# The first layer's turns: tap products in pairs, norms by VectorE's 32x32 transposes, TensorE's order fixed in the source

## The chip, the cores and the metric

The kernel runs on one core of one Trainium2 chip. The time is that of the device, in microseconds, for one launch. Engines are named as in the profile: PE is TensorE's matmuls, PEld its weight loads, DVE is VectorE, ACT is ScalarE, POOL is GpSimd, SP is SyncE, which issues DMAs here.

## The reference

The kernel computes a network of four attention layers over two images of 512 channels and 64x64 pixels in float32. Only the first layer matters here. It has eight heads of 64 channels, and each pixel attends to its 3x3 neighbourhood and to a pooled copy of the image at once. Cut to what is computed:

```python
x = group_norm(x)
q = l2norm(x @ W_q + b_q)                    # per head of 64 channels
qs = (q + query_embedding) * softplus(temperature)
k, v = split(x @ W_kv + b_kv);  k = l2norm(k)
local  = [sum_d qs * k[y + dy, x + dx] for 9 taps (dy, dx)]
pooled = qs @ l2norm(k_pool).T               # k_pool, v_pool from gelu(x @ W_sr) pooled by 4
a = softmax(concat(local, pooled))
a_local = a[:9] + q @ learnable_tokens + learnable_bias
out = (sum_taps a_local * v[y + dy, x + dx] + a[9:] @ v_pool) @ W_proj + b_proj
```

## The kernel before

Channels lie on the 128 partitions. The image's 512 channels are four chunks, its 4096 pixels four units of 1024, so the layer has 16 units for each image, numbered chunk by chunk. A chunk holds two heads. A block is 512 pixels (`TB`).

`Local.run` goes through turns i = -4 to 16. Each turn gives every stage another unit: keys are projected for unit i + 4, queries for i + 3, values and tap sums for i + 1 ("ahead"), attention is done for i, and the weighted sum of the nine neighbours for i - 1. A stage is a generator, and `in_turn` steps all of them round robin, one `yield` at a time; so the yields set the order of the source. The order in which each engine executes is not the source's: the tile framework's scheduler orders every engine's instructions, with the source's order as priority, and with what it takes to be ready. PSUM banks come from a pool (`bank()`, tiles called `mm`); who takes a bank next waits for the last reader of its content.

The stages, with the lines of before:

- `projections`: two 512-pixel blocks each of keys, queries and values: four matmuls of 128x128 by 512 for each (L134), ScalarE adds the bias and makes the squares.
- `norms`: four matmuls (L2276) sum the squares of up to four blocks over each head, with column groups of 32, so the rows of one PSUM bank hold two heads for each of the four. ScalarE copies them (L2279), TensorE transposes them (L2283, four times 128x128), VectorE takes inverse roots by Newton's steps on 32 columns (L2290 to L2298, into `wide`), TensorE transposes back (L2304), ScalarE copies (L2306).
- `normed`: a matmul spreads each head's scale over its 64 channels (L2318), VectorE multiplies keys (in the padded frame `kx`) and queries by it (L2326). Then `learned` makes the learnable part of the query (L2339).
- `tap_products`: VectorE multiplies the queries by the keys shifted by each of the nine taps, 128x1024 each (L2366), into a ring of three buffers `prods`.
- `tap_sums`: for each tap two matmuls of 128x32 (one for each block, L2379) sum a product over each head. Tap parity and block choose one of four column groups of 32 in one bank; ScalarE takes the exponentials.
- `attend`: scores against the pooled keys (L2411, two heads each), their exponentials (L2415), values (L2421), sums in halves added by GpSimd (L2426) and then over all (L2433, L2437), the reciprocal (L2458), and the local weights, which go to DRAM by the `rows` DMAs.
- `weigh`: for each tap a DMA brings the weights back, spread over channels (`rows` to `big` or `tap`), ScalarE copies them to PSUM (L2491), VectorE multiplies by the shifted values (L2499), GpSimd adds (L2504), and the sum goes to `yd` in DRAM (L2510).
- `fetch_output` and `output`: in the last turns the output projection reads `yd` back (L2199).

SyncE has one queue for these DMAs, in the order of its instructions. Turns 0 to 2 have no value blocks to project: units 0 to 3 of the values are made in turns -4 to -2 (the first chunk). Turns -4 to -1 only fill the pipeline, turns 12 and 13 project no keys, 13 no queries either, and 14 to 16 drain it and do the output. The pooled heads are worked out in turns -4 and -3.

Of the kernel before, what the change touches and what calls it, by code (L numbers as in the profile page):

```python
# [1914 lines left out]
class Local:  # L1915
# [9 lines left out]
    def __init__(self, net, X, Y, sp_scale, d, wp, yp, pp, ppt, pps):  # L1925
# [20 lines left out]
        self.prods = [whole.take([P, self.UT])] + [new([P, self.UT], f"prod{i}") for i in range(2)]  # L1946
# [19 lines left out]
        self.qn = new([P, self.UT], "qn")  # L1966
# [3 lines left out]
        self.wide = new([P, NT, P], "wide")  # L1970
# [12 lines left out]
        nc.gpsimd.memset(self.wide, 0.0)  # L1983
# [11 lines left out]
    def run(self):  # L1995


        self.nmean = self.net.stats[:, 0]
        xs = self.pooled_tokens()
        heads = self.pooled_heads(xs)  # L2000
        units = KC * self.UN
        unit = lambda u: u if 0 <= u < units else None
        self.pending = []
        for i in "qkv":
            self.fetch(i, 0)
        for i in range(-4, units + 1):
# [12 lines left out]
            values = ([ahead] if i >= self.UN - 1 and ahead is not None  # L2019
                      else {-4: [0], -3: [1, 2], -2: [3]}.get(i, []))  # L2020
            stages.append(self.projections(k, q, values, streams))
            stages.append(self.normed(ended))
            if i < -2:
                stages.append(islice(heads, 12 if i == -4 else None))
            if i == units - 3:
                stages.append(self.fetch_output())
            if i > units - 3:
                stages.append(self.output(i - units + 2))
            in_turn(*stages)

        self.nc.sync.dma_start(self.next_w, self.d["w_q1"].rearrange("(kc p) o -> p kc o", p=P))
        in_turn(self.output(KC - 1))
# [136 lines left out]
    def fetch_output(self):  # L2169

        for _ in range(3):

            yield
# [6 lines left out]
    def output(self, c4):  # L2180
# [4 lines left out]
        toks = ([self.prods[0], self.prods[1], self.prods[2], self.qs[(units - 2) % 3]] if c4 % 2  # L2185
# [46 lines left out]
    def projections(self, uk, uq, uvs, streams):  # L2232
# [23 lines left out]
        for step in range(10):  # L2256
            if step >= 6:
                project((uk, uq)[step // 2 - 3], "kq"[step // 2 - 3], step % 2)
            if step % 3 == 0 and values:
# [6 lines left out]
    def norms(self, streams, ended):  # L2266
# [11 lines left out]
        rows = wp.tile([P, TB], F32, name="n_rows")  # L2278
        nc.scalar.copy(rows, ps)  # L2279
        yield  # L2280
        ps = self.bank()
        for t in range(NT):
            nc.tensor.transpose(ps[:, t * P:(t + 1) * P], rows[:, t * P:(t + 1) * P],  # L2283
                                self.net.ident)


        sums = ps.rearrange("p (t s r) -> p t s r", t=NT, s=4)
        n, a = (sums[:, :, :, 2 * i:2 * i + 2] for i in range(2))
        y = wp.tile([P, NT, 4, 2], F32, name="roots")
# [4 lines left out]
        for i in range(3):  # L2294
            nc.vector.tensor_tensor(a, n, y, ALU.mult)
            nc.vector.tensor_tensor(a, a, y, ALU.mult)
            dst = self.wide.rearrange("p t (s r) -> p t s r", s=4)[:, :, :, :2] if i == 2 else y
            nc.vector.scalar_tensor_tensor(dst, a, 1.5, y, ALU.add, ALU.mult)  # L2298
        yield
        yield  # L2300
        yield
        ps = self.bank()
        for t in range(NT):
            nc.tensor.transpose(ps[:, t * P:(t + 1) * P], self.wide[:, t, :], self.net.ident)  # L2304
        rows = wp.tile([P, TB], F32, name="n_rows")
        nc.scalar.copy(rows, ps)  # L2306
# [3 lines left out]
    def normed(self, ended):  # L2310

        nc = self.nc
        for _ in range(5):
            yield
        for which in "kq":
# [11 lines left out]
            yield  # L2327
        if mine:
# [27 lines left out]
    def tap_products(self, u):  # L2356
# [5 lines left out]
        qs = qs.rearrange("p (y x) -> p y x", x=W)  # L2362
        y = u % self.UN * self.UY
        for k in range(9):
            dy, dx = divmod(k, 3)
            self.nc.vector.tensor_tensor(  # L2366
                self.prods[k % 3].rearrange("p (y x) -> p y x", x=W), qs,
                self.kx[:, y + dy:y + dy + self.UY, dx:dx + W], ALU.mult)
            yield

    def tap_sums(self, u):
# [3 lines left out]

        def sums(k):
            for j in range(2):
                q = 2 * j + k % 2
                nc.tensor.matmul(ps[32 * q:32 * q + 32, :],  # L2379
                                 self.cst[:, C_TAPW + 16 - 2 * k:C_TAPW + 48 - 2 * k],  # L2380
                                 self.prods[k % 3][:, j * TB:(j + 1) * TB], start=(k < 2),
                                 stop=(k > 6))
# [15 lines left out]
    def attend(self, u):  # L2398
# [45 lines left out]
        yield  # L2444
        values(0)
        yield
# [5 lines left out]
        yield  # L2452
# [9 lines left out]
        nc.vector.tensor_tensor(el, el, self.lt.pop(u), ALU.add)  # L2462
        self.spread = self.rows()
# [237 lines left out]
```

## Time and profile before

| | us |
|---|---|
| median of 3 runs | 5164.23 (5158.23 to 5171.0) |
| the profiled execution, its own time | 5163.61 |
| span of the profiled execution | 5161.7 |
| mean granted TensorE clock | 0.979 |
| VectorE busy | 3067.8 (59%) |
| ScalarE busy | 1863.1 (36%) |
| first-layer turns -3 to 13, first image | 194.6 to 904.0 |

In the windows table a row is one stretch of time, with each engine's busy time and number of instructions, the granted clock (1.00 is full), the share of the DMA engines and what they moved. In a group's line come the source line, engine, operation, what is written and read, shapes and count, then the busy time and the mean duration of one in ns, then the engine's idle time just before them and what ended it. A logical float32 matmul shows as two records. Turns are cut here where the first L2276 of each starts: 194.6, 232.3, 256.9, 290.4, 326.9, 370.5, 419.7, 463.5, 508.3, 552.6, 599.0, 642.7, 686.8, 730.5, 774.5, 818.2 and 860.9 us for i = -3 to 13.

### The profile page before, as it was taken

To read this page: it belongs to the slowest core of one execution; us is meant where nothing else is said; L and a number is where in the kernel's file an instruction comes from. 1 tells how busy PE (TensorE), PEld (TensorE's weight loads), DVE (VectorE), ACT (ScalarE), POOL (GpSimd) and SP (SyncE) were. 2 spreads that over 40 slices of the span, in tenths; PEclk is the share of its full clock that TensorE was granted. 3 is DMA by queue.
4 is the path that set the end of the run, shared out by engine and by line. 5 is a ranking of instruction groups with operands and counts; after the bars stand their busy time and mean duration, and the time that the engine had idled before them with its cause. 6 is when DMAs were issued, how large, how long until landed. Compare 5 with 4: busy or idle time off the path is not lost. (4 is left out here: it accounts for less than half of the span.)

```text
span 5161.7 us, 48736 instructions
## 1 busy us (share of the span) xinstructions
PE 4898.0 (95%) x17299; PEld 2034.4 (39%) x17299; DVE 3067.8 (59%) x3986; ACT 1863.1 (36%) x3547; POOL 1844.2 (36%) x1216
## 2 busy tenths in 40 slices
PE   7999999899999999999999999998999999999998
PEld 3423332555334444433344333325543344444333
DVE  4266777644579633478732677776446795334766
ACT  1245565324323233322112555652343232333221
POOL 0035566500420045454500455555013201454554
PEclk9999999999999999999999999999999999999999
DMA  3025556600000000211110355565000000000111
GB/s 149 2 78 137 144 140 171 173 27 10 1 1 17 1 1 1 66 52 49 58 70 3 96 142 140 143 168 163 19 10 1 2 15 1 1 1 21 39 46 44
DMA packets 124752, 309.88 MB, mean 60 GB/s; under 512 B 20882, under 2 KB 33682, under 8 KB 122964
## 3 DMA queue, kind: packets, MB, share of 16 engines
q1 hardware_dynamic: 124500, 306.68, 21.0%
q8 instruction: 139, 2.28, 0.2%
q14 instruction: 113, 0.93, 0.1%
HBM read 258.11 MB, written 48.50 MB: 59 GB/s over the span
## 5 line engine op out<-in xcount | busy, mean ns | idle before, releaser
L134 PE MATMUL mm<-big,w 128*128 128x512 f32 x2496 | 1162.5, 610 | 9.2 <-DVE late L2458 9.2
L134 PEld LDWEIGHTS mm<-big,w 128*128 128x128 f32 x2496 | 455.9, 192 | 677.0 <-issue 559.0
L2504 POOL TENSOR_TENSOR late<-late,big 128x1024 f32<-128x1024 f32 x192 | 454.1, 2365 | 196.4 <-DVE big L2499 178.8
L1616 POOL TENSOR_TENSOR big<-big 128x512 f32<-128x512 f32 x224 | 277.3, 1270 | 219.8 <-ACT big L1607 219.8
L2426 POOL TENSOR_TENSOR late<-late 128x512 f32<-128x512 f32 x128 | 160.6, 1276 | 514.6 <-ACT late L2415 492.6
L2499 DVE TENSOR_TENSOR big<-big,mm 128x512 f32<-128x512 f32 x384 | 255.9, 683 | 124.5 <-ACT mm L2491 104.5
L2491 ACT COPY mm<-big 128x512 f32<-128x512 f32 x428 | 244.8, 593 | 174.0 <-DMA big<-rows 140.3
L1607 ACT ACTIVATE big<-mm,ed 128x256 f32<-128x256 f32 x512 | 193.6, 489 | 232.8 <-DVE top L1603 200.4
L2504 POOL TENSOR_TENSOR late<-late,tap 128x1024 f32<-128x1024 f32 x96 | 227.1, 2366 | 101.1 <-DVE tap L2499 97.8
L1420 POOL TENSOR_TENSOR wq<-prob 128x512 f32<-128x512 f32 x48 | 70.8, 1498 | 506.6 <-ACT prob L1417 506.6
L1871 PE MATMUL mm<-k,w 128*128 128x512 f32 x512 | 236.8, 606 | 12.3 <-DVE k L1864 7.3
L1603 DVE TENSOR_REDUCE top<-mm 128x1 f32<-128x512 f32 x256 | 159.1, 684 | 148.5 <-PE mm L1535 148.5
L134 PE MATMUL mm<-big,wq 128*128 128x512 f32 x512 | 235.2, 609 | 2.7 <-ACT off_t L1219 2.7
L2366 DVE TENSOR_TENSOR prod<-qs,big 128x1024 f32<-128x1024 f32 x192 | 230.7, 1217 | 8.7 <-PE tap L2379 7.0
L1191 PE MATMUL mm<-big,wo 128*128 128x512 f32 x512 | 234.7, 604 | 0.0
L1581 PE MATMUL mm<-w,big 128*128 128x512 f32 x512 | 234.5, 601 | 0.0
L1346 PE MATMUL acc<-big,diag 128*128 128x512 f32 x512 | 226.5, 601 | 4.6 <-ACT diag L1344 4.6
L1861 DVE RECIPROCAL psD<-psD 128x512 f32<-128x512 f32 x64 | 215.1, 3362 | 1.9
L969 POOL TENSOR_TENSOR group_stats<-group_stats,cst 128x1 f32<-128x1 f32 (+1 forms) x20 | 12.1, 621 | 570.2 <-DVE group_stats L968 538.7
L2379 PE MATMUL tap<-prod,cst 128*32 128x512 f32 x768 | 198.3, 602 | 8.9 <-DVE prod L2366 8.0
L134 PE MATMUL mm<-big,big 128*128 128x512 f32 x464 | 201.7, 594 | 0.5 <-DVE b_sr L1007 0.5
L1417 ACT ACTIVATE prob<-mm 128x512 f32<-128x512 f32 x256 | 133.0, 603 | 171.6 <-PE mm L1414 171.4
(410 smaller groups left out, 8477.2 us busy)
## 6 DMA issues: line engine op xcount, KB each, us to landing
big<-rows SPq DMA_DIRECT2D x428, 256.0 KB, 4.3
tap<-rows SPq DMA_DIRECT2D x212, 256.0 KB, 4.2
yd<-late SPq DMA_DIRECT2D x32, 512.0 KB, 2.9
lost_all<-lost SPq DMA_DIRECT2D x128, 128.0 KB, 3.1
out<-big SPq DMA_DIRECT2D x64, 256.0 KB, 2.0
big<-in_W_kv SPq DMA_DIRECT2D x8, 1024.0 KB, 9.4
rows<-late SPq DMA_DIRECT2D x64, 128.0 KB, 2.3
big<-yd SPq DMA_DIRECT2D x16, 512.0 KB, 5.1
```

The source lines that it names most:

```text
L134: self.nc.tensor.matmul(ps, w[:, kc, :], X[:, kc, blk * TB:(blk + 1) * TB], start=(kc == 0), stop=(kc == KC - 1))
L1191: nc.tensor.matmul(ps, w[:, kc, oc * P:(oc + 1) * P], att[:, kc, :], start=(kc == 0), stop=(kc == KC - 1))
L1346: nc.tensor.matmul(accs[b], dg, src[:, b * TB:(b + 1) * TB], start=(j == 0), stop=(j == 6))
L1581: nc.tensor.matmul(ps, X[:, kc, lo:lo + P], wv[:, kc, :], start=(kc == 0), stop=(kc == KC - 1))
L1616: nc.gpsimd.tensor_tensor(a, a, part, ALU.add)
L1861: nc.vector.reciprocal(psD, psD)
L1871: nc.tensor.matmul(ps, self.wo[:, kc, oc * P:(oc + 1) * P], qs[:, kc, :], start=(kc == 0), stop=(kc == KC - 1))
L2366: self.nc.vector.tensor_tensor(self.prods[k % 3].rearrange("p (y x) -> p y x", x=W), qs, self.kx[:, y + dy:y + dy + self.UY, dx:dx + W], A ...
L2379: nc.tensor.matmul(ps[32 * q:32 * q + 32, :], self.cst[:, C_TAPW + 16 - 2 * k:C_TAPW + 48 - 2 * k], self.prods[k % 3][:, j * TB:(j + 1) * ...
L2491: nc.scalar.copy(ps, part)
L2499: nc.vector.tensor_tensor(part.rearrange("p (y x) -> p y x", x=W), self.vx[:, y:y + self.UY // 2, dx:dx + W], ps.rearrange("p (y x) -> p y ...
L2504: nc.gpsimd.tensor_tensor(out, out, t, ALU.add)
```

## The change

All of it is in the class `Local`, the first layer. Tap products are made two at a time: one VectorE instruction of 128x2048 for two taps, its keys read through an access pattern that steps from one tap's shift to the next's, and its queries read twice; the ninth tap stays alone. The ring is now two buffers of two products. The tap sums follow in pairs. In `norms`, both sets of TensorE transposes and both ScalarE copies go; VectorE transposes the 32x32 blocks of the sums in place in PSUM, does the same thirteen steps, and transposes back into the buffer `sq[3]` (whose squares were read by then). `wide` goes, and `qn` moves to the large buffer. In turns 0 to 13 TensorE's instructions run in the source's order; the other engines are still ordered by the scheduler. The yields are moved: values are projected at steps 0, 2, 5 and 9, keys and queries at 4, 6, 7 and 8; `normed` begins two steps earlier and learns one step later; the values of the first score group come one step later and of the second one step earlier, the rows' DMA one step later, and the output's fetch after 7 steps rather than 3.

The lines of after that answer to those of before: sums of squares L2279, first VectorE transpose L2282, the steps L2285 to L2292, second transpose L2294, scale matmul L2306, multiply L2314, learnable part L2328, products L2353, tap sums L2380, scores L2404, values L2414, reciprocal L2450, tap multiply L2492, tap add L2497.

```diff
@@ run
-            in_turn(*stages)
+            if 0 <= i < units - 2:
+                with self.net.tc.manual_schedule(engines={mybir.EngineType.PE}):
+                    in_turn(*stages)
+            else:
+                in_turn(*stages)
...
@@ __init__
-        self.prods = [whole.take([P, self.UT])] + [new([P, self.UT], f"prod{i}") for i in range(2)]
+        self.prods = [new([P, 2, self.UT], f"prods{i}") for i in range(2)]
-        self.qn = new([P, self.UT], "qn")
+        self.qn = whole.take([P, self.UT])
-        self.wide = new([P, NT, P], "wide")
-        nc.gpsimd.memset(self.wide, 0.0)
...
@@ fetch_output
-        for _ in range(3):
+        for _ in range(7):
...
@@ projections
         for step in range(10):
-            if step >= 6:
-                project((uk, uq)[step // 2 - 3], "kq"[step // 2 - 3], step % 2)
-            if step % 3 == 0 and values:
+            if step in (4, 6, 7, 8):
+                i = (4, 6, 7, 8).index(step)
+                project((uk, uq)[i // 2], "kq"[i // 2], i % 2)
+            if step in (0, 2, 5, 9) and values:
@@ norms
-        rows = wp.tile([P, TB], F32, name="n_rows")
-        nc.scalar.copy(rows, ps)
-        yield
-        ps = self.bank()
-        for t in range(NT):
-            nc.tensor.transpose(ps[:, t * P:(t + 1) * P], rows[:, t * P:(t + 1) * P],
-                                self.net.ident)
-        sums = ps.rearrange("p (t s r) -> p t s r", t=NT, s=4)
-        n, a = (sums[:, :, :, 2 * i:2 * i + 2] for i in range(2))
-        y = wp.tile([P, NT, 4, 2], F32, name="roots")
+        yield
+        nc.vector.transpose(ps, ps)
+        n, a = (ps.rearrange("p (b r) -> p b r", r=32)[:, :, 2 * i:2 * i + 2] for i in range(2))
+        y = wp.tile([P, TB // 32, 2], F32, name="roots")
...
-            dst = self.wide.rearrange("p t (s r) -> p t s r", s=4)[:, :, :, :2] if i == 2 else y
-            nc.vector.scalar_tensor_tensor(dst, a, 1.5, y, ALU.add, ALU.mult)
-        yield
-        yield
-        yield
-        ps = self.bank()
-        for t in range(NT):
-            nc.tensor.transpose(ps[:, t * P:(t + 1) * P], self.wide[:, t, :], self.net.ident)
-        rows = wp.tile([P, TB], F32, name="n_rows")
-        nc.scalar.copy(rows, ps)
+            nc.vector.scalar_tensor_tensor(n if i == 2 else y, a, 1.5, y, ALU.add, ALU.mult)
+        rows = self.sq[3]
+        nc.vector.transpose(rows, ps)
@@ normed
-        for _ in range(5):
+        for _ in range(3):
             yield
...
             yield
+        yield
         if mine:
             self.learned(mine[-1][0][3])
@@ tap_products
-        for k in range(9):
-            dy, dx = divmod(k, 3)
+        for k in range(0, 9, 2):
+            n = min(2, 9 - k)
             self.nc.vector.tensor_tensor(
-                self.prods[k % 3].rearrange("p (y x) -> p y x", x=W), qs,
-                self.kx[:, y + dy:y + dy + self.UY, dx:dx + W], ALU.mult)
-            yield
+                self.pair(u, k)[:, :n].rearrange("p k (y x) -> p k y x", x=W),
+                bcast(qs.rearrange("p (y x) -> p y x", x=W), 1, n),
+                self.shifted(u % self.UN * self.UY, k, n), ALU.mult)
+            yield
+            if n == 2:
+                yield
+    def pair(self, u, k):
+        return self.prods[(5 * u + k // 2) % 2]
+    def shifted(self, y, k, n):
+        a = self.kx[:, y:y + self.UY, :W]
+        at = lambda k: k // 3 * (W + 2) + k % 3
+        part, rows, cols = a.ap
+        return bass.AP(a.tensor, a.offset + at(k), [part, [at(k + 1) - at(k), n], rows, cols])
@@ tap_sums
-        yield
-        yield
-        for k in range(0, 8, 2):
-            sums(k)
-            sums(k + 1)
-            yield
-            if k < 6:
+        yield
+        for k in range(0, 9, 2):
+            for i in range(min(2, 9 - k)):
+                for j in range(2):
+                    q = 2 * j + i
+                    nc.tensor.matmul(ps[32 * q:32 * q + 32, :],
+                                     self.cst[:, C_TAPW + 16 - 2 * (k + i):][:, :32],
+                                     self.pair(u, k)[:, i, j * TB:(j + 1) * TB],
+                                     start=(k == 0), stop=(k + i > 6))
+            for _ in range((2, 2, 3, 1, 0)[k // 2]):
                 yield
-        sums(8)
@@ attend
         exponentials(0, 1)
         yield
+        yield
         values(0)
-        yield
         exponentials(1, 0)
...
         values(1)
-        yield
         yield
         psD = sums()
...
         nc.vector.tensor_tensor(el, el, self.lt.pop(u), ALU.add)
+        yield
         self.spread = self.rows()
```

More of the change, by code (lines that the diff above doesn't have):

```diff
@@ L2184, in output @@
         units = KC * self.UN
-        toks = ([self.prods[0], self.prods[1], self.prods[2], self.qs[(units - 2) % 3]] if c4 % 2
+        toks = ([a[:, i] for a in self.prods for i in range(2)] if c4 % 2
                 else [self.kraw, self.qn,
@@ L2361, in tap_products @@
             self.nc.scalar.copy(qs[:, part], self.qs[u % 3][:, part])
-        qs = qs.rearrange("p (y x) -> p y x", x=W)
-        y = u % self.UN * self.UY
-        for k in range(9):
-            dy, dx = divmod(k, 3)
+        for k in range(0, 9, 2):
+            n = min(2, 9 - k)
             self.nc.vector.tensor_tensor(
-                self.prods[k % 3].rearrange("p (y x) -> p y x", x=W), qs,
-                self.kx[:, y + dy:y + dy + self.UY, dx:dx + W], ALU.mult)
+                self.pair(u, k)[:, :n].rearrange("p k (y x) -> p k y x", x=W),
+                bcast(qs.rearrange("p (y x) -> p y x", x=W), 1, n),
+                self.shifted(u % self.UN * self.UY, k, n), ALU.mult)
             yield
+            if n == 2:
[7 more added lines that the diff above has]
+        return bass.AP(a.tensor, a.offset + at(k), [part, [at(k + 1) - at(k), n], rows, cols])
     def tap_sums(self, u):
@@ L2374, in tap_sums @@
         ps = self.ppt.tile([P, TB], F32, name="tap")
[L2376 to L2382, printed above, removed]
-        yield
-        yield
-        for k in range(0, 8, 2):
-            sums(k)
-            sums(k + 1)
-            yield
-            if k < 6:
+        yield
+        for k in range(0, 9, 2):
[7 more added lines that the diff above has]
+            for _ in range((2, 2, 3, 1, 0)[k // 2]):
                 yield
-        sums(8)
         el = self.els()
```

## The prediction

> **What bounds the kernel now.** I read the busy times of the page first, then the time of each turn of the first layer (the table of windows, cut where the first matmul of L2276 starts), then the groups by shape, and last the order of TensorE's work inside two turns (the timeline).
>
> ```profile
> PE 4898.0 (95%) x17299; PEld 2034.4 (39%) x17299; DVE 3067.8 (59%) x3986; ACT 1863.1 (36%) x3547; POOL 1844.2 (36%) x1216
> ```
>
> TensorE is the bound overall, and only the first layer's turns change: 195 to some 1035 us for the first image, and the same from 2756 us for the second.
>
> ```profile
> core 0: us, PE busy (x) PEld busy (x) DVE busy (x) ACT busy (x) POOL busy (x), PEclk, DMA share, GB/s
> 326.90:370.50 43.60, 41.10 (x155) 12.46 (x150) 32.66 (x52) 25.80 (x46) 26.24 (x13) 1.00 0.47 132
> 370.50:419.70 49.20, 45.59 (x159) 14.17 (x159) 35.47 (x55) 26.68 (x47) 26.22 (x13) 0.97 0.56 146
> 419.70:818.20 398.50, 395.93 (x1437) 132.03 (x1436) 286.86 (x449) 241.27 (x423) 235.27 (x117) 1.00 0.55 141
> 818.20:860.90 42.70, 40.62 (x153) 12.71 (x155) 34.84 (x53) 24.21 (x43) 26.51 (x13) 0.96 0.74 194
> 860.90:904.00 43.10, 39.16 (x149) 11.07 (x148) 32.12 (x50) 24.34 (x43) 27.09 (x14) 0.96 0.66 180
> ```
>
> The third row is nine steady turns (i = 3 to 11) of 44.28 us, TensorE busy for 99%: there only TensorE work removed, or a new wait, counts. Turns 1 and 2 (rows one and two) have no value projections, yet are no shorter: they wait. So do 12 and 13 (the last two). In 326.9 to 419.7 the waits of TensorE are on VectorE: L2304 for L2298 3.4 us in all, L2379 for the products of L2366 2.3.
>
> ```profile
> L2379 PE MATMUL tap<-prod,cst 128*32 128x512 f32 x768 | 198.3, 602 | 8.9 <-DVE prod L2366 8.0
> L2366 DVE TENSOR_TENSOR prod<-qs,big 128x1024 f32<-128x1024 f32 x192 | 230.7, 1217 | 8.7 <-PE tap L2379 7.0
> L2318 PE MATMUL mm<-n_rows,cst 2*128 2x512 f32 x256 | 75.6, 653 | 10.4 <-ACT n_rows L2306 10.2
> L2304 PE MATMUL mm<-cst,wide 128*128 128x128 f32 x136 | 22.4, 288 | 9.4 <-DVE wide L2298 9.0 <-DVE kp L2162 0.4
> L2283 PE MATMUL mm<-cst,n_rows 128*128 128x128 f32 x136 | 22.3, 286 | 2.2 <-ACT n_rows L2279 2.2
> L1142 DVE TENSOR_TENSOR big<-big,wkv 128x2048 f32<-128x2048 f32 x12 | 27.4, 2282 | 0.3
> L1799 DVE TRANSPOSE_TENSOR_REDUCE sq_cols<-sq 128x16 f32<-128x512 f32 x64 | 43.9, 694 | 26.8 <-POOL sq L1504 26.0 <-PE mm L1810 0.7
> L1861 DVE RECIPROCAL psD<-psD 128x512 f32<-128x512 f32 x64 | 215.1, 3362 | 1.9
> ```
>
> **What TensorE saves.** A matmul's duration overlaps the next, so I count from start to start in steady turns. The two groups of four transposes (L2283, L2304) take 0.585 and 0.587 us: 1.17 us a turn go. The tap sums run in four column groups of 32, so four matmuls (eight records) take 0.997 us together, while a lone tap's two take 0.952. Before, they are issued as they come and cost 5.77 us a turn; the change issues four full groups and one lone tap: 4 x 0.997 + 0.952 = 4.94, 0.83 less. Two projection blocks that ran back to back (7.06 for the pair) now stand alone (3.63 each): 0.2 more. The best steady turns last 43.7 us: 43.7 - 1.17 - 0.83 + 0.2 = 41.9 us. Adding up the groups of the new order gives 41.6. I take 41.75 before any wait.
>
> **What VectorE gets.** Nine products of 1024 a turn become four of 2048 and one of 1024: L1142 has 2.28 us for 2048, L2366 1.217 for 1024, about 0.1 us saved for each pair. Two block transposes of 128x512 in PSUM come in. The trace has none; L1799, which transposes and reduces the same shape, takes 0.694. From below nothing is cheaper than a 128x32 step (0.19), from above stands the dearest VectorE row of the shape, L1861 (3.36). I take 0.69. ScalarE loses two copies of 0.58 a turn, which lay beside TensorE and are only worth their latency. The norm chain thus loses eight transposes and two copies. VectorE's order around it (first transpose, thirteen steps of 0.1 to 0.2 with some adds and a product of 2.2 among them, second transpose) gives 8.4 us, start to start: 2 x 0.7, thirteen steps by 0.225 where each waits for the last (2.9), a product (2.2) and three adds of L2499 (0.6 each). TensorE's order gives the clock: a score group (L2411) 1.06, a value block 3.63, the sums of squares (L2276) 1.0, so the first transpose starts at 5.8 us and the scales are there at 14.2. TensorE goes on with scores 1.06, two taps 1.0, a value block 3.63, values (L2421) 1.87, scores 1.06, two taps 1.0, and asks for them at 15.3. It fits with 1.1 us to spare.
>
> [...]
>
> **The wait it adds.** TensorE's order is now the source's: after taps 2 and 3 come the k norms (after's L2306) 1.06, a score group 1.06, then the first k projection, due at 17.42. Its PSUM bank is the one that the k norms leave when VectorE's first multiply by them (after's L2314) is done. On VectorE that multiply is queued behind the product of taps 6 and 7, which rewrites the buffer that taps 2 and 3 read until 15.3 us. So: 15.3 + 0.1 latency + 2.20 product + 0.60 add + 0.69 multiply + 0.05 = 18.94 us: 1.5 us of wait a turn. Behind it on TensorE stands all the rest of the turn, and for that nearly every other engine. I found no other wait over 0.2 us: the sums want GpSimd's halves at 26.3 us, and they come at 25.5 to 26.1.
>
> Such a wait has a second price, in the timeline (start, length, and in brackets the idle time before):
>
> ```profile
> 566.65 1.94 PE L2421 MATMUL mm<-late,vp 128*64 128x512 f32 x8
> 569.65 1.13 PE L2318 MATMUL mm<-n_rows,cst 2*128 2x512 f32 x4 [1.07 <-ACT n_rows L2306]
> 570.71 5.40 PE L134 MATMUL mm<-big,w 128*128 128x512 f32 x8
> 576.04 1.13 PE L2318 MATMUL mm<-n_rows,cst 2*128 2x512 f32 x4
> ```
>
> After 1.07 us without work the next projection block takes 5.33 us to the start of the next, where others take 3.63; the turn's granted clock is 0.96. That is 1.7 us; other waits of 1 to 1.8 us passed without it. I put it in four turns of ten: 0.65 us.
>
> [...]
>
> Steady turn after: 41.75 + 1.5 + 0.65 = 43.9 us, 0.4 less than 44.28; nine turns: 3.5 us for each image.
>
> **The other turns.** Turns 1 and 2 took 92.8 us together. Without value blocks the groups sum to 34.3 us a turn, and the norm chain (2.5 us late at TensorE), the same wait of 1.4 us and a clock drop make it 38 to 40; with the 3.6 us of the block that stands before the next cut: 80 to 84. I take 8.5 us less. Turns 12 and 13 took 85.8 and have no k norms to wait for; the last, without them and without k projections, comes to 38 or 39 each: I take 7.5 less. Turn 0: 36.5 becomes 35. Turns -3 to -1, in the scheduler's order still, lose transposes and the waits at L2304 and L2318: 1 us each, 3 in all. The output turns (904 to 1035 us) wait on reads of yd and on weights, now fetched four steps later in the turn: between 4 less and 4 more, I take 0. The rows' DMA is issued one step later, but its two tap fetches stand ahead of the write of yd (L2510) in SyncE's queue, not behind it: some 5 us earlier, so GpSimd's adds (nine of 2.36 and four of 1.27, 26.3 of 44 us) keep 2 to 3 us of slack. Were that cover gone, the loop's own period, 42.7 to 43.1 as in turns 12 and 13, would still lie below 43.9.
>
> Sum: 3.5 + 8.5 + 7.5 + 1.5 + 3 = 24 us less an image, 48 for two, less 2 for the second image's slightly fewer waits: 46. The profiled execution took 5163.61 us (span 5161.7, 1.9 around it), 0.6 below the median of 5164.23: forecast 5118.
>
> **Rivals.**
> *No wait.* If VectorE frees the bank in time (a shorter product, or another bank), the steady turn is 41.75: 22.5 us an image in place of 3.5, 84 in all, some 5080 us. For it: VectorE is busy 32 of 44 us. Against: the order above, in which the multiply can't pass the product. Chance 0.2.
> *Half clock each turn, and the weigh loop.* The wait comes at one place in each turn; if the clock falls each time, the turn is 44.95, 6 us an image lost instead of 3.5 gained, and turns 1, 2, 12 and 13 keep half: 5140 to 5165. For it: of the four waiting turns in the table three have 0.96 or 0.97. Against: turn 1 waits 2.5 us in pieces and has 1.00. Chance 0.2.
> *Slower: VectorE's transposes.* The fixed order puts all of TensorE behind L2294 (after). If each transpose costs t rather than 0.69, the chain ends 2(t - 0.69) later, of which 1.1 is free. With 24 us an image to lose over nine turns (2.65 each), the change loses from t = 2.6. At 3.36, L1861's price, the wait is 4.2 us more a turn and the later one partly overlaps it: nine turns by 4.2 to 5.5, twice, less 48: 30 to 50 us slower, 5193 to 5215. For it: the operation is not in the trace, and it works in place in PSUM. Against: L1799 reads the same tile, transposed, in 0.694. Chance 0.15.
>
> **How the numbers follow.** Forecast 0.45 (5100 to 5140). With the first rival and a third of the second: faster 0.72. A measurement tells 0.3%, 15.5 us, from no change: faster is below 5148.7, slower above 5179.7. The rest of the second rival: same 0.13; the third: slower 0.15. Range 5078 to 5182: from the first rival's end to where the third begins.
>
> **What would show it.** Right: L2282 and L2294 near 0.7, L2353 at 2.28; the steady turn 43.5 to 44.2; among TensorE's waits, one of L134 for L2314, about 1.5 us, in nearly each steady turn; turns 1 and 2 at about 84 together. Wrong: a steady turn below 42.5 (no wait), waits of L2306 for L2294 in steady turns (transposes dear), or a clock of 0.96 or lower in all of them.

## The result, and the profile after

The changed kernel takes 5174.26 us (median of 10 runs, 5160.23 to 5179.74), before 5155.95 (10 runs, 5148.03 to 5171.0). The ratio is 1.0028 [1.0016, 1.0039]: it got slower by 0.28%, where 0.9% faster was forecast. The profiled execution took 5175.17 us with a span of 5173.3, 11.6 more than before's. The page's first rows, and its groups of the new operations:

```profile
span 5173.3 us, 48047 instructions
PE 4874.0 (94%) x17027; PEld 2003.3 (39%) x17027; DVE 3104.9 (60%) x3926; ACT 1818.8 (35%) x3479; POOL 1845.5 (36%) x1214
```

```profile
L2282 DVE STREAM_TRANSPOSE mm<-mm 128x512 f32<-128x512 f32 x34 | 24.8, 730 | 108.1 <-PE mm L2279 108.1
L2294 DVE STREAM_TRANSPOSE sq<-mm 128x512 f32<-128x512 f32 x34 | 24.4, 716 | 1.6
L2353 DVE TENSOR_TENSOR prods<-qs,big 128x2048 f32<-128x2048 f32 x128 | 292.3, 2287 | 86.8 <-PE tap L2380 76.3 <-ACT qs L2350 10.2
```

TensorE has 24 us less busy time, as meant; the transposes cost 0.73 and 0.72 us (0.69 was taken), the pair 2.287 (2.28). Each price was right. The windows, cut where the first L2279 starts (turns 1, 2, 3 to 11, 13, and the output):

```profile
core 0: us, PE busy (x) PEld busy (x) DVE busy (x) ACT busy (x) POOL busy (x), PEclk, DMA share, GB/s
321.00:368.40 47.40, 41.27 (x142) 12.31 (x144) 33.03 (x49) 24.34 (x44) 25.82 (x13) 0.86 0.48 125
368.40:417.60 49.20, 43.09 (x146) 13.17 (x144) 35.46 (x51) 25.89 (x47) 26.59 (x14) 0.90 0.51 139
417.60:819.20 401.60, 386.61 (x1369) 121.13 (x1368) 300.00 (x432) 228.53 (x405) 236.10 (x117) 1.00 0.52 140
858.70:904.00 45.30, 39.48 (x144) 11.31 (x144) 32.29 (x47) 22.86 (x40) 26.55 (x13) 0.89 0.68 189
904.00:1035.00 131.00, 118.23 (x288) 64.12 (x287) 89.62 (x142) 43.13 (x81) 70.19 (x35) 0.90 0.63 173
```

Nine steady turns are busy for 386.6 us instead of 395.9, and take 401.6 instead of 398.5: TensorE stands idle for 15 us where it had stood for 3. In turns 1, 2, 13 and the output the granted clock is 0.86 to 0.90, where it was 0.93 to 1.00. The row of the output before:

```profile
904.00:1035.00 131.00, 116.20 (x288) 67.56 (x288) 90.89 (x147) 43.09 (x79) 72.27 (x37) 0.93 0.61 170
```

Summed over both images, from the marks of the turns:

| | before | after | difference | forecast |
|---|---|---|---|---|
| turns -3 to -1 | 190.3 | 182.7 | -7.6 | -6 |
| turn 0 | 73.0 | 73.0 | 0 | -3 |
| turns 1 and 2 | 185.7 | 192.7 | +6.9 | -17 |
| turns 3 to 11 | 797.3 | 803.2 | +5.9 | -7 |
| turn 12 to the next layer's first matmul (L981) | 511.7 | 518.6 | +6.9 | -15 |

The rest, in which no line is changed, makes -0.5.

The record of the clock accounts for a good part of it. From turn -3 to L981 the clock is at half speed for 44.4 us in the first image and 51.2 in the second before, and for 82.4 and 78.5 after: 65 us more, 34 of them in turns 1 and 2 and 31 from turn 12 on, none in turns 3 to 11. At half clock a group of scales took 2.01 us to the next start (L2306 at 336.25 us of after) instead of 1.05 (at 615.20), so these 65 us are worth up to 33 (an estimate) of the 58 between the forecast (46 less) and the profile (11.6 more). It isn't the profiled execution alone: the mean clock is 0.972 to 0.976 in the ten runs of after, and 0.976 to 0.983 in the 27 runs of before taken beside e1.

**Inside a steady turn** (timeline of TensorE, start, length, idle time before in brackets):

```profile
611.57 3.70 PE L134 MATMUL mm<-big,w 128*128 128x512 f32 x8 [1.49 <-DVE big L2314]
615.20 1.13 PE L2306 MATMUL mm<-sq,cst 2*128 2x512 f32 x4
616.25 1.94 PE L2414 MATMUL mm<-late,vp 128*64 128x512 f32 x8
618.12 1.07 PE L2380 MATMUL tap<-prods,cst 128*32 128x512 f32 x8
619.12 2.86 PE L2426 MATMUL mm<-late,cst 128*64 128x512 f32 x8
621.91 1.08 PE L2430 MATMUL mm<-late,cst 64*64 64x512 f32 x4
```

The first line is the wait that the prediction named, at its size (1.49 us for 1.5). The fifth is one that it missed: the eight records take 2.79 us to the next start, where before they took 1.87. The idle time lies inside the group, so no bracket shows it. GpSimd's two half sums explain it:

```profile
618.33 2.52 POOL L2419 TENSOR_TENSOR late<-late 128x512 f32<-128x512 f32 x2 [2.38 <-PE mm L2414]
```

They write over what the values (L2414, to 618.19) read, so they can't start earlier, and end at 620.85; the second half of L2426 starts at 620.91.

**Inside turn 1**, TensorE waits longest for the norms:

```profile
328.51 1.82 PE L2404 MATMUL mm<-big,kp 64*128 64x512 f32 x4 [1.43 <-DVE big L2492]
330.26 1.93 PE L2380 MATMUL tap<-prods,cst 128*32 128x512 f32 x8
336.25 2.08 PE L2306 MATMUL mm<-sq,cst 2*128 2x512 f32 x4 [4.06 <-DVE sq L2294]
338.26 2.08 PE L2404 MATMUL mm<-big,kp 64*128 64x512 f32 x4
340.27 5.50 PE L134 MATMUL mm<-big,w 128*128 128x512 f32 x8
```

VectorE's timeline of the same stretch shows why:

```profile
330.93 0.19 DVE L2292 SCALAR_TENSOR_TENSOR roots<-mm,roots 128x32 f32<-128x32 f32 x1
331.15 0.20 DVE L2290 TENSOR_TENSOR mm<-mm,roots 128x32 f32<-128x32 f32 x1
332.26 2.29 DVE L2353 TENSOR_TENSOR prods<-qs,big 128x2048 f32<-128x2048 f32 x1 [0.91 <-PE tap L2380]
334.47 0.19 DVE L2291 TENSOR_TENSOR mm<-mm,roots 128x32 f32<-128x32 f32 x1
334.57 0.68 DVE L2492 TENSOR_TENSOR big<-big,mm 128x512 f32<-128x512 f32 x1
335.16 0.19 DVE L2292 SCALAR_TENSOR_TENSOR mm<-mm,roots 128x32 f32<-128x32 f32 x1
335.39 0.72 DVE L2294 STREAM_TRANSPOSE sq<-mm 128x512 f32<-128x512 f32 x1
```

In turns 1 and 2 the scheduler put the product of taps 6 and 7 inside the third Newton step. It can't start before TensorE's taps 2 and 3 (330.26), and the two engines wait for each other in turn. The clock's record has half speed for 13.65 us from 330.3 and for 10.24 us from 378.1: the 2.08 above is the length of 1.13 at half clock, and the 5.50 that of 3.70 with half clock for its first 3.6 us.

### The profile page after: what moved, and what is told of

It reads as the page before. It is cut to its first block, busy times and chain, and to the rows that moved or that the text cites. A ratio compares the mean times of both kernels' runs of the same rounds, so it can differ in the third digit from the quotient of the medians.

```text
span 5173.3 us, 48047 instructions
## 1 busy us (share of the span) xinstructions
PE 4874.0 (94%) x17027; PEld 2003.3 (39%) x17027; DVE 3104.9 (60%) x3926; ACT 1818.8 (35%) x3479; POOL 1845.5 (36%) x1214
## 5 line engine op out<-in xcount | busy, mean ns | idle before, releaser
L134 PE MATMUL mm<-big,w 128*128 128x512 f32 x2496 | 1176.8, 614 | 35.3 <-DVE big L2314 26.8
L134 PEld LDWEIGHTS mm<-big,w 128*128 128x128 f32 x2496 | 456.5, 193 | 720.9 <-issue 594.7
L2497 POOL TENSOR_TENSOR late<-late,big 128x1024 f32<-128x1024 f32 x192 | 455.1, 2370 | 230.6 <-DVE big L2492 216.5
L2353 DVE TENSOR_TENSOR prods<-qs,big 128x2048 f32<-128x2048 f32 (+1 forms) x160 | 331.4, 2074 | 105.8 <-PE tap L2380 95.3
L2492 DVE TENSOR_TENSOR big<-big,mm 128x512 f32<-128x512 f32 x384 | 251.3, 680 | 54.8 <-ACT mm L2484 54.5
L2497 POOL TENSOR_TENSOR late<-late,tap 128x1024 f32<-128x1024 f32 x96 | 226.6, 2360 | 125.7 <-DVE tap L2492 121.4
L134 PE MATMUL mm<-big,wq 128*128 128x512 f32 x512 | 236.5, 611 | 2.7 <-ACT off_t L1219 2.7
L134 PE MATMUL mm<-big,big 128*128 128x512 f32 x464 | 201.7, 594 | 0.5 <-DVE b_sr L1007 0.5
L2380 PE MATMUL tap<-prods,cst 128*32 128x512 f32 x1152 | 182.0, 628 | 14.1 <-DVE prods L2353 14.1
```

Of the source, the lines that this page charges most:

```text
L134: self.nc.tensor.matmul(ps, w[:, kc, :], X[:, kc, blk * TB:(blk + 1) * TB], start=(kc == 0), stop=(kc == KC - 1))
L2353: self.nc.vector.tensor_tensor(self.pair(u, k)[:, :n].rearrange("p k (y x) -> p k y x", x=W), bcast(qs.rearrange("p (y x) -> p y x", x=W), ...
L2492: nc.vector.tensor_tensor(part.rearrange("p (y x) -> p y x", x=W), self.vx[:, y:y + self.UY // 2, dx:dx + W], ps.rearrange("p (y x) -> p y ...
L2497: nc.gpsimd.tensor_tensor(out, out, t, ALU.add)
```

## The experiments

A table first, by kind of matmul: the mean time of a steady turn (turns 3 to 11, both images), from the start of each TensorE instruction to the start of the next, so that a wait is charged to the group ahead of it. The last column is the time at half clock in one turn.

| us a turn | turn | projections | taps | scores | values | scales | transposes | half sums | half clock |
|---|---|---|---|---|---|---|---|---|---|
| before | 44.29 | 21.78 | 5.77 | 4.52 | 4.10 | 2.12 | 1.24 | 1.87 | 0.38 |
| after | 44.62 | 21.97 | 5.21 | 5.80 | 3.73 | 2.12 | 0 | 2.79 | 0.38 |
| e1 scheduled | 44.48 | 21.59 | 5.90 | 4.37 | 3.63 | 2.12 | 0 | 3.88 | 0 |
| e2 taps later | 44.25 | 21.80 | 5.48 | 4.55 | 3.73 | 2.85 | 0 | 2.83 | 1.14 |
| e3 and projection | 44.41 | 22.00 | 5.94 | 5.06 | 3.73 | 2.81 | 0 | 1.87 | 2.84 |
| e4 norms alone | 44.69 | 21.59 | 6.90 | 4.45 | 4.54 | 2.41 | 0 | 1.87 | 0 |
| e5 pairs alone | 45.24 | 21.96 | 5.82 | 4.94 | 4.34 | 2.12 | 1.30 | 1.87 | 0.95 |
| e6 filled | 44.35 | 21.79 | 5.35 | 4.60 | 3.74 | 4.00 | 0 | 1.87 | 0 |
| e7 thin fill | 45.87 | 22.21 | 5.93 | 5.16 | 3.73 | 3.97 | 0 | 1.87 | 3.60 |
| e9 order G | 45.93 | 22.51 | 4.97 | 7.14 | 3.73 | 2.71 | 0 | 1.87 | 1.33 |
| e16 short fill | 43.93 | 21.84 | 5.66 | 4.69 | 3.73 | 3.15 | 0 | 1.87 | 0 |
| e17 block as cover | 45.09 | 21.96 | 5.43 | 5.43 | 5.31 | 2.12 | 0 | 1.87 | 0.38 |

Sums of squares, the last four matmuls of the sums and the learned part (2.9 to 3.0 together) hardly move. In e6, e7 and e16 the fill that they add is counted under scales.

**e1, the order alone undone.**

```diff
-            if 0 <= i < units - 2:
-                with self.net.tc.manual_schedule(engines={mybir.EngineType.PE}):
-                    in_turn(*stages)
-            else:
-                in_turn(*stages)
+            in_turn(*stages)
```

> After, but TensorE's order in turns 0 to 13 left to the scheduler again; pairs and VectorE's transposes stay. Theory W (the gain is eaten by two waits that the fixed order makes in each steady turn, 1.49 us of the first k projection for L2314 and 0.9 us inside the sums group L2426 for GpSimd's halves, and by 4 us of waits with half clock in each of turns 1 and 2): the scheduler moves other work into those places, steady turn 42.5 to 43.5 us instead of 44.43, 15 to 45 us faster than after. Rival V (VectorE's new work, 2.29-us products and transposes, is what costs, whatever TensorE's order): turn 44.0 to 44.6, within 8 us of after.

Measured: 5156.63 us, ratio to before 1.0004 [0.9989, 1.0019], 0.24% (12 us) less than after's ratio; steady turn mostly 44.11, 44.48 in the mean. The total lies between the two, nearer to theory W's 15 to 45 us than to rival V's 8; the turn is where rival V had it: the waits for the multiplies (L2314 in after) are rare (1.1 us in nine turns), but the half sums take 3.88. Pairs and norms together bring nothing even under the scheduler.

**e2 and e3, the two waits taken away.**

```diff
-            for _ in range((2, 2, 3, 1, 0)[k // 2]):
+            for _ in range((3, 1, 3, 1, 0)[k // 2]):
# e3 also:
-            if step in (4, 6, 7, 8):
-                i = (4, 6, 7, 8).index(step)
+            if step in (4, 5, 7, 8):
+                i = (4, 5, 7, 8).index(step)
```

> After with taps 2 and 3 summed one step later, so that the k norms (L2306) stand ahead of them on TensorE, and the product of taps 6 and 7 falls behind the k multiplies (L2314) in VectorE's queue, in steady turns as in turns 1 and 2. Theory W: the wait of L134 for L2314 goes (9 times 1.5 us an image), turns 1 and 2 lose the 4-us waits for L2294 and most of their half clock: steady turn 42.9 to 43.1, turns 1 and 2 about 40 each, some 45 to 55 us less than after in all. Rival V or a rival loop (another period, of GpSimd, the DMAs or VectorE, sets 44.4 us): the turn stays at 44.2 to 44.5, with the wait in another place.

> As e2_taps_later, and the second k projection moved from behind the sums group (L2426) to ahead of it, so that GpSimd has 4.6 us for its halves rather than 1.0. Theory W: the 0.9 us inside L2426 goes as well: steady turn 41.9 to 42.3, some 60 to 75 us less than after. Rival loop: no shorter than e2_taps_later.

Measured: 1.0016 [1.0001, 1.0032] and 1.0023 [1.0012, 1.0033]. Both waits went: nothing waits for L2314, and in e3 the half sums are at 1.87. But the turn stayed at 44.25 and 44.41. A new wait came, 0.73 us inside the k norms (scales 2.85 and 2.81): the second k norm's bank had just been filled with the third scores, and it starts at 609.48 us, when ScalarE's first exponential of them ends (609.42). And in e3 the clock falls in eight of nine turns of the first image. Its timeline (the second line is the group with the wait; from 611.07 to 614.48 the clock is half):

```profile
607.61 1.13 PE L2404 MATMUL mm<-big,kp 64*128 64x512 f32 x4
608.73 1.86 PE L2306 MATMUL mm<-sq,cst 2*128 2x512 f32 x4
610.53 1.58 PE L2404 MATMUL mm<-big,kp 64*128 64x512 f32 x4
612.04 1.94 PE L2380 MATMUL tap<-prods,cst 128*32 128x512 f32 x8
613.90 3.97 PE L134 MATMUL mm<-big,w 128*128 128x512 f32 x8
```

The half-clock stretches of 3.41 us start at 433.6, 477.9, 522.3, 566.7, 611.1, 699.8, 744.2 and 788.6 us: 44.4 apart (once twice that), 13 times 3.413. A turn of e3 without one takes 42.75. So these starts lie on one grid of 3.413 us, the step that the clock's records of before and after show as well; an e3 turn with a loss of about 1.6 us (44.4 for 42.75) is 13 steps long, so that the next turn met the grid at the same place and mostly lost again.

**e4 and e5, each part alone on the before kernel.** e4 puts the VectorE transposes into before's `norms`, e5 the pairs into its `tap_products` and `tap_sums`, both as in the change's diff.

> Before with VectorE's block transposes in the norms as the only change (single products, scheduler's order). Theory W: TensorE loses 1.17 us of transposes a turn and nothing waits for it: steady turn 43.0 to 43.3 instead of 44.28, 15 to 30 us faster than before. Rival V: VectorE's 1.45 us of transposes delay products and the norm chain: turn 44.2 or more, within 8 us of before or slower.

> Before with the tap products in pairs as the only change (TensorE's transposes and the scheduler's order stay; to make room, the norms' row copies and the transposed roots lie in two of the buffers sq). By the prediction's sum, full groups of four tap matmuls: taps 5.0 to 5.3 us a turn instead of 5.77, steady turn 43.5 to 43.9, 5 to 15 us faster than before. Rival (as e4 showed for the norms: the scheduler's order of TensorE loses in other groups what is saved): turn 44.2 or more, within 8 us of before or slower.

Measured: 1.0038 [1.0025, 1.0052] and 1.0050 [1.0034, 1.0067], each slower than before by itself. In e4 the transposes go (1.24) and their price comes back in taps (6.90 for 5.77), values (+0.44) and scales (+0.29): with VectorE's order changed, the scheduler left 36 single tap matmuls alone in the 18 turns (20 before, some 0.96 us each), and eight groups of seven take 3.35 us where before's of six take 1.84. In e5, too, the taps don't get cheaper under the scheduler's order, and scores and values cost more (+0.42 and +0.24). e5's norms use the buffers `sq` for their rows, and 4.0 us in nine turns are waits of L2317 on that copy; so a part of its loss is of that making. So the groups that the scheduler placed couldn't be costed one by one here.

**e6 and e7, the wait filled.**

```diff
+            if which == "k" and len(mine) == 2:
+                for i in range(2):   # e6; e7: self.cst[:2, C_ROW:C_ROW + P], self.cst[:2, :TB]
+                    nc.tensor.matmul(mine[0][1], self.net.ident, self.cst[:, :TB], start=True, stop=True)
```

> e3 with two idle-filling matmuls of 128x128 by 512 ahead of the first k norm, whose result the k norm overwrites. In e3 the second k norm waits 0.74 us for the bank of the scores before it, and the granted clock is 0.5 for 3.41 us in nearly each steady turn. Theory K (the wait, in a stretch of narrow matmuls, lowers the clock, which costs 1.5 us): with the wait filled the clock stays at 1.00 and the turn gets shorter, 42.7 to 43.1 us instead of 44.41, in spite of 0.9 us more work. Rival loop (another engine's period holds the turn at 44.4): 44.3 to 44.6.

> As e6_filled, but with the two filling matmuls using 2 rows of the array, like the norms. If the clock looks at whether TensorE is busy: as e6_filled, 42.7 to 43.1 us. If it looks at how much of the array works: half clock in most turns as in e3, 44.2 to 44.5.

Measured: e6 1.0015 [0.9999, 1.0030], e7 5213.72 us in its one run. The fill was mis-sized: a 128x128 by 512 matmul in float32 takes 0.91 us (two records; a block of four takes 3.63), so 1.81 for two (1.88 in e6's turn at 607.04 us), not 0.9. So e6's turn is 43.9, and 44.35 in the mean. But its clock is whole. e7 has the same order and fill time (scales 3.97 and 4.00). Windows of e6, then e7, turns 3 to 11:

```profile
418.30:819.80 401.50, 397.09 (x1409) 125.77 (x1410) 300.36 (x433) 233.61 (x406) 239.21 (x117) 1.00 0.54 140
```

```profile
423.80:838.70 414.90, 411.53 (x1405) 130.72 (x1404) 300.81 (x434) 233.83 (x406) 239.01 (x117) 0.96 0.52 136
```

The two kernels differ only in the operands of the two matmuls: 128 rows of the array with the identity as weights, or 2 rows with other weights. With 128 the clock stayed at 1.00 in these turns; with 2 it was half for 3.6 us a turn (0.96 in the mean), though TensorE is busy for 411.5 of 414.9 us. In the 3.41 us ahead of each of the six falls of the first image only scores (64 rows), scales and fill (2 rows each) run, and TensorE is busy for 3.07 to 3.41 us of them. So idle time alone didn't set the clock in these two runs: e7 has less of it (3.4 us against 4.4) and the lower clock. The operands of the fill made the difference; whether by the rows of the array or by the weights that go with them, the two runs don't show.

**e8, values between.** The third scores are issued ahead of the first values.

> e3 with the first values group (L2414) moved behind the third score group, so that 1.87 us of work stand between those scores and the k norms that take their banks. Theories W and K: no wait over 0.3 us and no half clock in steady turns, 41.8 to 42.3 us, 40 us less than e3 in all. Rival loop: 44.3 to 44.6.

Measured: 1.0030 [1.0014, 1.0045]; turn 44.03 in the mean, 43.70 mostly, no half clock. The k norms' wait went, but values took 4.74. The exponentials lie in a ring of four, so this order makes the first values read those of the third scores: it changes the result's pooled part for that half, and it makes them wait. That wait is of the experiment's own making, so e8 decides nothing about a turn without waits.

**e9 and e10, another order (G).** The sums of squares come 3.6 us earlier, and no product stands inside VectorE's norm chain; stages are listed as `tap_products, tap_sums, normed, attend, norms, weigh, projections`.

> After in another fixed order (order G), made from what e2 to e8 showed: the sums of squares a step earlier (after the first scores), the k norms ahead of values, third scores and taps 2 and 3, the second k projection ahead of the sums group. VectorE's norm chain then has 4 us more and no product inside it, the k multiplies stand ahead of the product of taps 6 and 7, GpSimd has 4.6 us for its halves, and no bank is asked for just after its reader starts. Theories W and K (waits on in-order queues, and the half clock that follows them, eat the gain): steady turn 41.7 to 42.4 us, hardly any half clock in it, turns 1 and 2 below 43 each, 35 to 75 us faster than before. Rival loop (each wait that is removed comes back elsewhere, since another engine's period holds the turn): 43.6 to 44.5 and no faster than before.

> Order G, with TensorE's order fixed only in turns 0 to 11; turns 12 and 13 are left to the scheduler. If the fixed order of turns 12 and 13 is what costs after the drain (turn 12 to the end of the layer 259 us against 253 to 255 without it): 3 to 8 us less an image than e9; if the drain is bound by yd and the output in any case: within 3 us an image of e9.

Measured: 1.0120 [1.0098, 1.0141] and 1.0087 [1.0066, 1.0109]: far off. The wait of L134 for the multiplies is back (13.4 us in nine turns), 10.4 us are waits for exponentials, and scores take 7.14. The rival is nearer, in that removed waits returned; but there was no common period: turns of 45 and 47 us alternate. From turn 12 to L981 e10 takes some 2 us an image less than e9 (265.1 against 267.4 in the first).

**e11, the order fixed in turns 3 to 11 only.**

> After with TensorE's order fixed in turns 3 to 11 only. Turns 1 and 2 (VectorE's queue has the product of taps 6 and 7 inside the norm chain, TensorE waits 4 us for it and half clock follows): if the fixed order is their cause, they fall from 96.5 to below 92 together; if the pairs and the scheduler's order of VectorE are (e1 has 95.6 there without any fixed order), they stay at 94 to 97. Drain as in e1, 4 us an image less than after. In all 5 to 20 us faster than after.

Measured: 1.0009 [0.9996, 1.0023]. Turns 1 and 2 together: 94.4 and 93.5 us for the two images, against 96.6 and 96.1 after. So of the 3.8 and 3.1 us that these turns lose against before, 2.2 and 2.6 are of TensorE's fixed order. But they don't get below before without it: e1 has 95.6 and 92.6, before 92.8 and 93.0. The rest of the forecast gain is missing with either order. Turn 12 to L981: 254.9 and 261.2, after 259.0 and 259.5; no clear gain.

**e12 to e15, seven banks.** The copy of the queries to PSUM goes, `mm` gets its two banks:

```diff
-        qs = self.pps.tile([P, self.UT], F32, name="qs")
-        for j in range(2):
-            part = slice(j * TB, (j + 1) * TB)
-            self.nc.scalar.copy(qs[:, part], self.qs[u % 3][:, part])
+        qs = self.qs[u % 3]
...
-                tc.tile_pool(name="l0m", bufs=5, space=PSUM) as pp, \
+                tc.tile_pool(name="l0m", bufs=7, space=PSUM) as pp, \
```

> After with seven PSUM banks for the pool mm instead of five: the tap products read the scaled queries where they lie in SBUF, not from a copy in two banks (ScalarE's two copies, L2350, go). Theory B (banks: the fixed order asks for a bank before VectorE or ScalarE has read it): the 1.5-us wait of L134 for L2314 goes, the wait of the sums for GpSimd's halves (0.9 us, no bank) stays; steady turn 42.6 to 43.2 us instead of 44.43. Rival loop: 43.7 to 44.5 with waits of another kind. If reading both operands from SBUF slows the products, L2353 rises above 2.29 us.

> As e12, the queries read from SBUF, but still five banks. Theory B: the wait for L2314 is there again, steady turn 44.2 to 44.7 like after. If ScalarE's copies mattered and not the banks: like e12.

> Before with seven banks and the queries read from SBUF. Theory B: the scheduler found other work for the few bank waits, 0.3 us a turn to gain: steady turn 43.5 to 44.4, within 10 us of before in the turns 3 to 11; the other turns may gain 2 to 5 us each. Rival loop: no change at all.

> e3 (taps 2 and 3 later, second k projection ahead of the sums) with seven banks and the queries read from SBUF. Theory B with K: neither the wait of the second k norm for the scores' bank nor the half clock that it brings; steady turn 41.6 to 42.3 us instead of 44.41, 40 to 60 us faster than e3. Rival loop: 43.7 or more.

Measured: 1.0155 [1.0134, 1.0176], 5263.81 us in one run, 1.0145 [1.0124, 1.0166] and 1.0140 [1.0115, 1.0164]. The reading from SBUF spoiled the test. Groups of e12, from 419 to 820 us:

```profile
L2349 DVE TENSOR_TENSOR prods<-big 128x2048 f32<-128x2048 f32 x36 | 112.4, 3122 | 12.6 <-PE tap L2376 12.6
L2415 POOL TENSOR_TENSOR late<-late 128x512 f32<-128x512 f32 x34 | 68.9, 2049 | 42.5 <-PE mm L2410 25.5 <-ACT late L2404 17.0
L2493 POOL TENSOR_TENSOR late<-late,big 128x1024 f32<-128x1024 f32 x51 | 131.9, 2586 | 63.3 <-DVE big L2488 61.5
```

The pair costs 3.12 us instead of 2.29, GpSimd's halves 2.05 instead of 1.28, its adds 2.59 instead of 2.36: the two engines held each other up. The 18 pair products of e12 that no work of GpSimd overlaps take 2.25 to 2.29 us, the other 110 up to 4.49. e14's taps take 9.04 us a turn (turn 47.20), and e15 (46.62) waits 18.8 us in nine turns for the second transpose, so neither says what the banks are worth. Between e13 and e12, which differ in the banks alone, the wait of L134 for L2314 (19.3 us in eight turns) goes, and waits of L134 for L2488 (16.0 in eight) take its place; the turn falls from 48.1 to 47.4. So that wait is one for a bank, but two banks more are worth only 0.8 us here.

**e16 and e17, with the order fixed in turns 3 to 11 only.** e16 is e3 with half the fill (`[:, :TB // 2]`), e17 moves the second value block to step 3 and taps 2 and 3 to step 5.

> e3 with two filling matmuls of 128x128 by 256 (0.9 us; those of e6 took 1.81) ahead of the first k norm, and TensorE's order fixed in turns 3 to 11 only. Theory W and K: the 0.73-us wait for the scores' bank is filled, the clock stays whole: steady turn 42.8 to 43.2 us instead of 44.41 in e3, 15 to 30 us faster than before. Rival loop: 43.7 to 44.5.

> After with the second value block (3.6 us of needed work) between the third scores and the k norms, taps 2 and 3 after the second values and taps 4 and 5 a step later, the second k projection ahead of the sums, and TensorE's order fixed in turns 3 to 11 only. By hand each bank is then free when asked for, the k multiplies are not behind a product, GpSimd's halves have 4.6 us, and only 0.3 us of wait for the exponentials of the second scores is left. Theories W and K: steady turn 41.9 to 42.6 us, no half clock in it, 30 to 50 us faster than before. Rival loop: 43.7 or more.

Measured: e16 0.9993 [0.9981, 1.0006], e17 1.0040 [1.0025, 1.0055]. Nine of e16's 18 turns take 43.05 us, as W and K said, without half clock; the mean is 43.93:

```profile
417.70:814.80 397.10, 391.80 (x1425) 126.61 (x1424) 304.24 (x436) 234.54 (x407) 239.46 (x117) 1.00 0.55 145
```

The other nine take 0.7 to 3.6 us more; in the one from 680.4 us it is 0.85 inside the scores group that follows the sums of squares and 0.4 ahead of a projection. e17 failed at a new place: the third scores now wait for a bank that VectorE's Newton step reads:

```profile
606.87 1.13 PE L2404 MATMUL mm<-big,kp 64*128 64x512 f32 x4 [1.51 <-DVE roots L2292]
608.71 3.70 PE L134 MATMUL mm<-big,w 128*128 128x512 f32 x8 [0.71 <-ACT late L2408]
```

No version was measurably faster than before; e16 is level with it.

## Why the prediction was wrong

*What TensorE saves* held in the main. The groups sum to 41.6: e16's undisturbed turn of 43.05 is that sum with 1.03 of fill and 0.17 of a wait for ScalarE, to within 0.25. In after the transposes give 1.24, the taps only 0.56 of the 0.83 forecast.

*What VectorE gets* held in its prices, and so the third rival (dear transposes) fell: 0.72, far from the 2.6 at which it would have decided.

*The wait it adds* held at 1.49 us. The step that failed here is "I found no other wait over 0.2 us". The half sums were placed by the time of a turn without waits; they hang on the second values, whose operand they overwrite, so in each steady turn of after's first image they end 2.66 or 2.67 us after them, and the fixed order has 0.99 us of taps and 0.93 of the group's first half to put between. The missed 0.92 us, with 0.17 for ScalarE, outweighs the 0.65 put down for the clock (0.2 measured). Turn: 41.6 + 1.49 + 0.92 + 0.17 = 44.2, measured 44.43 in most and 44.62 in the mean, forecast 43.9. This term is 13 us of the 58 between forecast and profile.

*The other turns* failed most: 24 us in turns 1 and 2, 22 in turn 12 to the output. The sum for turns 1 and 2 used the order that VectorE has in the steady turns, with the product of taps 6 and 7 behind the norm chain. There it stands inside the chain, waits for TensorE, and TensorE for it: 4.06 us instead of 2.5, further waits (1.43 and 0.64 in turn 1, 1.9 in turn 2), and half clock for 13.65 and 10.24 us instead of one clock drop in each. The groups themselves were right: 72.2 us for both turns without waits (2 x 34.3 and 3.6), 12.2 of waits and 11.9 lost at half clock make 96.3, measured 96.6; the prediction had 8 to 12 for waits and clock together. e2, which moves that product behind the k multiplies, took turn 1 from 47.3 to 44.5 us, but turn 2 only from 49.3 to 48.6: the norms are still waited for (2.9 us in each), and the clock in turn 2 is half for as long as in after (10.24 us). So the place of that product is shown to cost 3 to 3.5 us of some 12 an image; what else keeps the waits and the clock there stays open.

The gain in turn 12 came (39.5 and 39.0 for 42.6 and 44.9), and was given back from turn 13 to L981, which take 9.1 and 6.8 us more. The step that failed is that the sum has no term for the clock there. TensorE's waits are as long as before (22.2 and 23.7 us for 22.3 and 23.6); the time at half clock grew from 23.9 to 44.8 us and from 30.7 to 44.4, worth up to 10.5 and 6.8. Why the clock falls there wasn't tried, nor the fetch four steps later by itself; e1, e11, e16 and e17, which have that fetch but leave turn 12 and all behind it to the scheduler, take 253 to 261 us from turn 12 to L981, no less than before on the whole (253.1 and 258.7).

*The rivals.* "Half clock each turn" came in another place than it said: steady turns of after are nearly free of it (0.38 us a turn), e3's are full of it (2.84), and so are after's waiting turns (a granted clock of 0.86 to 0.90). It was priced at 5140 to 5165, since the waiting turns were still to gain half; they lost.

The length of the waits didn't tell where the clock falls: after's steady turns have a wait of 1.49 us and 0.38 us of half clock a turn, e3's 0.73 us without work and 2.84 of half clock, and e7 has half clock after stretches in which TensorE was hardly idle (busy for 3.07 to 3.41 of 3.41 us).

Why the scheduler packs the taps as it does in e4 and e5 wasn't tried. What the shortest turn could be with more banks stays open, since the test of it changed what VectorE and GpSimd read.

## What to carry to other kernels

An order fixed on one engine is priced against the queues of the others in each stretch, not in the steady one alone: here a product placed inside a chain on VectorE in two turns cost 3 to 3.5 us an image, as much as nine steady turns were to give. Sum the granted clock by stretch, too: here the time at half clock grew by 65 us, far beyond what the prediction had put down, worth up to 33 us (an estimate from half of these 65). Look for idle time inside groups (start to start against the group's best), since the list of waits leaves it out, and for operations that write over what another engine still reads: their start moves with that reader. In the steady turns, where TensorE was busy for 99%, work taken away turned into waits: for a bank that wasn't free when it was asked for (1.49 us a turn), and for GpSimd (0.92).

## What the runs showed of the hardware

- The granted clock differed between e6 and e7 (one run), which differ in the operands of two matmuls a turn alone: with 128 rows it was 1.00 in turns 3 to 11 (no half clock), with 2 rows 0.96 (3.6 us of half clock a turn), though TensorE was idle for 4.4 us of 401.5 in e6 and for 3.4 of 414.9 in e7.
- Half clock came in whole steps of 3.413 us on a fixed grid: in the traces of before (37 stretches) and after (45) all but the last, which the trace's end cuts, last 1 to 5 whole steps, and all start on one grid, to within 4 ns. In e3 eight stretches start 44.4 us apart (once twice that), 13 steps, the length of its turn.
- In e12, whose products read both operands from SBUF beside a busy GpSimd, the product of 128x2048 took 3.12 us in the mean, where after's, with one operand in PSUM, took 2.29, and GpSimd's 128x512 add 2.05 instead of 1.28. Without GpSimd's work beside it such a product of e12 took 2.25 to 2.29 us, with it up to 4.49.
- VectorE's 32x32 block transpose of 128x512 in float32 took 0.72 us from PSUM to SBUF (L2294 of after), in place in PSUM 0.73 (L2282).
